# Two ends of an attention and expert kernel: the first projections and the last group rearranged

## The chip, the cores and the metric

The kernel runs on one core of one Trainium2 chip. Its engines are TensorE (PE, with its weight loads as PEld), VectorE (DVE), ScalarE (ACT), GpSimd (POOL) and SyncE (SP), which only issues transfers. ACT and POOL issue transfers too. The metric is the device time of one execution in microseconds; the time before is 2715.6 us, the median of three runs (2714.85 to 2717.81). All times below are microseconds unless marked ns.

## The reference

For 32 sequences of 512 tokens and 256 channels, 16 heads of 16 channels, causal attention runs twice. The values are the input itself. The second attention takes its values from the first one's error.

```python
qk = x @ W_attn + b_attn
q, k = (qk[..., :C], qk[..., C:])          # v = x, by heads
y = _causal_attn(q, k, v)
e = v[:, :, 1:, :] - y[:, :, :-1, :]
k2 = (x[:, :-1] @ W_k2 + b_k2)
y2 = _causal_attn(q[:, :, 1:, :], k2, e)   # a row of zeros ahead
x = layernorm(x + proj(y) + proj(y2))
x = layernorm(x + ffn(x))                  # ffn: top-2 of 8 experts
```

The experts touch only the first 512 tokens, sequence 0. For the other 31 sequences the expert output added is nought, so the second norm follows the first directly.

## The kernel before

**Tiling.** Four heads make a group, four groups a sequence: 128 groups in all. Two neighbouring groups are projected together (`project`, L194 to L213): the products land in a PSUM bank, ACT adds a bias and writes `pk` (L210), POOL rounds it to `lead` (L212) and subtracts (L213), so that `lead` and `pk` hold a high and a low part. `spread` (L215) moves both to the layout of the score products, `q_t` and `kk_t`, by SBUF-to-SBUF transfers of 128 KB or halves of that on SP's queue.

**Steps.** `step(n)` (L631) is a pipeline over groups. It runs five slots. A slot multiplies queries and keys for the maxima of group n (`maxima`, reduced by DVE at L296), and for the exponentials of group n-1 (`scores`, exp by ACT at L353, the causal triangle cut by POOL at L357). After each slot come the functions in `rest[slot]`: `values` (products `av` at L400, drained by ACT at L408), `normalize` (transposes `yt` at L415, the division by DVE, and for the first attention POOL's `e_pad` at L440), projections of a later pair, the output projection (`turn` and `attended`, products `po` at L492), the experts of sequence 0, and loads and stores. `values(n, 0)` and `normalize(n, 0)` are the first attention of a group, `(n, 1)` the second.

**The last block.** For every sequence but 0, `attended(b, i)` adds the residual to block i of 128 rows (DVE, L495) and calls `twice_normed`: statistics by DVE (L507, L508), the factor r by POOL (L510, L511), the norm itself by POOL (L512). `store(b)` (L515) writes all four blocks as one transfer of 512 KB, eight steps after the sequence's end, or for the last sequence in step 131.

**What sets the order.** The instructions of PE and SP stand in the order of the code. Those of DVE, ACT and POOL are ordered by a scheduler when the kernel is built, and each engine then runs strictly in that order. In the start this has a consequence: the small work of `route` for the experts (load of `rws` by POOL at L526, `wt * rws` by DVE at L536) stands ahead of DVE's first maximum. PSUM has four single banks (`bank`) and two double ones; a new tile waits until the one that held its bank has been drained.

**Before the steps.** SP loads `xT` and the weights, ACT issues eight small bias loads (L102), `w_proj` and `b_proj`; DVE packs the weights (L108); POOL builds masks. Then pair 0 is projected and spread, the first x and its shifted copy xs are loaded (L175 to L183), and POOL makes two tiles of ones (L708, L712).

Of the kernel before, what the change touches and what calls it, by code (L numbers as in the profile page):

```python
# [9 lines left out]
F32 = mybir.dt.float32  # L10
# [3 lines left out]
AF = mybir.ActivationFunctionType  # L14
ALU = mybir.AluOpType
AX = mybir.AxisListType

P = 128
# [16 lines left out]
def half(ap):  # L35
    return ap.bitcast(F32R)
# [3 lines left out]
def block_kernel(  # L40
# [16 lines left out]
    nc = tc.nc  # L57
    B, T, C = x.shape
# [9 lines left out]
    const = ctx.enter_context(tc.tile_pool(name="const", bufs=1))  # L68
# [10 lines left out]
    def bank(name):  # L79
        return psum.tile([P, T], F32, tag="one", name=name, bufs=4)  # L80


    seqs = {}

    def load_turned(b):
# [82 lines left out]
    moving = {}  # L168

    def load(b):  # L170
        if b:
            load_turned(b)
        s = seqs[b]
        s["x"] = seq.tile([P, NB, C], F32, tag="x", name=f"x{b}")
        nc.sync.dma_start(s["x"], x[b].rearrange("(n p) c -> p n c", p=P))  # L175
# [18 lines left out]
    def project(two, m, lo=0, hi=T):  # L194
        b, part = divmod(two, NG // 2)
        ps = bank(f"pj{two}_{m}_{lo}")
        for c in range(NC):
            nc.tensor.matmul(  # L198
                ps[:, 0 : hi - lo],
                wq_sb[:, m, c, part * P : (part + 1) * P],  # L200
                seqs[b]["xT"][:, c, lo:hi],
                start=(c == 0),
                stop=(c == NC - 1),
            )
        if lo == 0:
            pk = work.tile([P, T], F32, tag=f"half{m}", name=f"pk{two}_{m}", bufs=1)
            lead = work.tile([P, T], F32, tag=f"lead{m}", name=f"lead{two}_{m}", bufs=1)
            moving[two, m] = lead, pk
        lead, pk = moving[two, m]
        nc.scalar.activation(pk[:, lo:hi], ps[:, 0 : hi - lo], AF.Identity, bias=bp_qk[:, m, part : part + 1])  # L210
        if hi == T:
            nc.gpsimd.tensor_copy(half(lead), pk)  # L212
            nc.gpsimd.tensor_sub(half(pk), pk, lead)  # L213

    def spread(two, m):  # L215

        for k in range(2):
            n = 2 * two + k
            d = groups.setdefault(n, {})
            d["q"] = q_t[n % len(q_t)]  # L220
            d["kk"] = kk_t[n % len(kk_t)]
            rows = slice(k * GH * HD, (k + 1) * GH * HD)
            for i, t in enumerate(moving[two, m]):
                if m == 0:
                    for r in range(2):
                        nc.sync.dma_start(d["q"][r::2, i], t[rows])
                else:
                    nc.sync.dma_start(d["kk"][i::2, m - 1], t[rows])
        del moving[two, m]

# [159 lines left out]
    def values(n, a):  # L392
        b, g = divmod(n, NG)
        d = groups[n]
        vals = (v_pad, e_pad)[a]
        ps = bank(f"av{n}_{a}")
        order = [0, 2, 1, 3] if a == 0 else [0, 1, 3, 2]
        for j in order:
            for h in range(GH):
                nc.tensor.matmul(  # L400
                    ps[HS * h : HS * (h + 1), j * P :],
                    vals[:, j, (g * GH + h) * HV : (g * GH + h) * HV + HS],
                    d["pt", a, j, h // NH2][:, h % NH2],
                    start=(j == order[0]),
                    stop=(j == order[-1]),
                )
        avs = d["avs", a] = work.tile([P, T], F32, tag="avs", name=f"avs{n}_{a}")
        nc.scalar.copy(avs, ps)  # L408
# [75 lines left out]
    def attended(b, i):  # L484

        s = seqs[b]
        if i == 0:
            pool = seq if b else const
            s["h"] = pool.tile([P, NB, C], F32, tag="h" if b else "h0", name=f"h{b}")
        ps = bank(f"po{b}_{i}")  # L490
        for c in range(NC):
            nc.tensor.matmul(  # L492
                ps[:, 0:C], s["ysT"][:, c, i * P : (i + 1) * P], wp_sb[:, c], start=(c == 0), stop=(c == NC - 1)
            )
        nc.vector.tensor_add(s["h"][:, i], ps[:, 0:C], s["xr"][:, i])  # L495
        if b:
            twice_normed(b, i)
        elif i == NB - 1:
            norm(s["h"], f"a{b}")

    def twice_normed(b, i):


        t = seqs[b]["h"]
        mv = small.tile([P, 2], F32, tag="mv2", name=f"mv{b}_{i}")
        stats = small.tile([P, nc.vector.BN_STATS_DIM], F32, tag="stats", name=f"st{b}_{i}")
        nc.vector.bn_stats(stats, t[:, i])  # L507
        nc.vector.bn_aggr(mv, stats)  # L508
        r = small.tile([P, 1], F32, tag="r2", name=f"r{b}_{i}")
        nc.gpsimd.tensor_scalar(r, mv[:, 1:2], 1.0 + EPS, EPS * EPS, ALU.mult, ALU.add)  # L510
        nc.gpsimd.tensor_tensor(r, r, mhalf[:, 0:1], ALU.pow)  # L511
        nc.gpsimd.tensor_scalar(t[:, i], t[:, i], mv[:, 0:1], r, ALU.subtract, ALU.mult)  # L512

    def store(b):
        nc.sync.dma_start(out[b].rearrange("(n p) c -> p n c", p=P), seqs.pop(b)["h"])  # L515
# [112 lines left out]
    n_all = B * NG  # L628
    first_expert = 2 * NG + 4

    def step(n):  # L631
        ready = lambda k: 0 <= k < n_all
        rest = [[] for _ in units]
        b, r = divmod(n, NG)
        if r == 1 and b + 1 < B:
            load(b + 1)
        if r == 3 and b + 1 < B:
            load_next(b + 1)
        if ready(n):
            prepare(n)  # L640
        if ready(n - 3):
            rest[3].append(lambda: normalize(n - 3, 1))
        if ready(n):
            rest[4].append(lambda: halve(n))
        if ready(n - 1):
            rest[0].append(lambda: augment(n - 1))
        if ready(n - 2):
            rest[1].append(lambda: values(n - 2, 0))
            rest[2].append(lambda: normalize(n - 2, 0))
            rest[4].append(lambda: values(n - 2, 1))  # L650
        two = n // 2 + 1
        if ready(2 * two):
            if n % 2 == 0:
                rest[2].append(lambda: project(two, 1))
                rest[4].append(lambda: spread(two, 1))
            else:
                rest[2] += [lambda: project(two, 0), lambda: spread(two, 0)]
                rest[0].append(lambda: project(two, 2, 0, T // 2))
                rest[3] += [lambda: project(two, 2, T // 2), lambda: spread(two, 2)]
        b, r = divmod(n - 3, NG)  # L660
        if r == NG - 1 and 0 <= b < B:
            rest[4].append(lambda b=b: turn(b))

        for b in range(B):
            end = (b + 1) * NG - 1
            last = b == B - 1
            for part in range(2):
                if n == (end + 4 if last else min(end + 5 + 2 * part, n_all)):
                    rest[0].append(lambda b=b, part=part: attended(b, 2 * part))
                    rest[3].append(lambda b=b, part=part: attended(b, 2 * part + 1))  # L670
                if n == (end + 3 if last else end + 4):
                    rest[1 + 2 * part].append(lambda b=b, part=part: biased(b, part))
            if n == (end + 2 if last else end + 3):
                rest[3].append(lambda b=b: load_residual(b))
            if b and n == (end + 4 if last else end + 8):
                rest[4 if last else 1].append(lambda b=b: store(b))


        e = n - first_expert
        if e == -1:  # L680
            rest[4] += [route, turn_tokens, lambda: load_hidden(0), lambda: load_down(0)]
        if e == 0:
            rest[0].insert(0, biases)
        if 0 <= e < E:
            rest[3].insert(0, lambda: hidden(e, 0, 0))
            rest[4].insert(0, lambda: hidden(e, 0, 1))
        if 0 <= e - 1 < E:
            rest[0].insert(0, lambda: hidden(e - 1, 1, 0))
            rest[1].insert(0, lambda: hidden(e - 1, 1, 1))
            rest[2].insert(0, lambda: down(e - 1))  # L690
            if e < E:
                rest[1].append(lambda: load_hidden(e))
                rest[2].append(lambda: load_down(e))
        if e == E:
            rest[4].append(lambda: second_norm(0, moe["acc"]))
        for s in range(len(units)):
            slot(n, s)
            for f in rest[s]:
                f()

    for m in range(3):
        project(0, m)
        spread(0, m)
    load(0)
    load_next(0)
    for a in range(2):
# [85 lines left out]
```

## Time and profile before

| | |
|---|---|
| median of the runs | 2715.6 |
| profiled execution, its own time | 2717.53 |
| its span | 2715.8 |
| PE busy | 2618.0 (96%) |
| DVE busy | 1933.8 (71%) |
| ACT busy | 1754.0 (65%) |
| POOL busy | 1733.0 (64%) |
| chain that ended last | PE 76%, ACT 14%, issue 3%, POOL 3%, DVE 2%, DMA 1% |

The span runs from the first to the last instruction; the profiled execution took 1.7 us longer than its span. The chain follows the work back from the last instruction to what released each step. A timeline line gives start, duration, engine and line, operation, output and input, and in brackets how long the engine had been idle and what ended it. "PEclk" is the clock that PE was granted, 1.00 being full.

### The profile page before, as it was taken

The numbers are of one execution on the slowest core, as the hardware profiler recorded it, in microseconds if no ns is written. First come the engines' busy times: TensorE is split into PE (matmuls) and PEld (weight loads), VectorE is DVE, ScalarE is ACT, GpSimd is POOL, SyncE is SP. The second block draws the span as 40 slices with busy tenths as digits, with TensorE's granted clock in tenths as the row PEclk, the third lists the DMA queues.
The fourth block names the chain that finished last, engine by engine and source line by source line (L and its number), as shares of the span: only waits on it lengthen the run. The fifth ranks groups of instructions, "written<-read, shape, count | busy, mean of one in ns | idle before, by whom it ended". The sixth has DMA issues, their size and how long they took to land.

```text
span 2715.8 us, 98001 instructions
## 1 busy us (share of the span) xinstructions
PE 2618.0 (96%) x41488; PEld 1786.1 (66%) x41488; DVE 1933.8 (71%) x3220; ACT 1754.0 (65%) x3412; POOL 1733.0 (64%) x3312
## 2 busy tenths in 40 slices
PE   6999999999999999999999999999999999999996
PEld 3666666666666666666666666666666666666664
DVE  5767777777777777777777777777777777777772
ACT  2666554566666666666666666666666666666663
POOL 4555555566666666666666666666666666666665
PEclk7999999999999999999999999999999999999998
DMA  5233223233233333333333333333333333333320
GB/s 137 70 74 99 68 86 89 77 80 101 81 85 90 87 96 80 97 85 80 95 85 97 80 100 83 78 97 85 98 80 97 86 78 97 84 99 79 97 55 24
DMA packets 166421, 233.25 MB, mean 86 GB/s; under 512 B 20472, under 2 KB 90112, under 8 KB 165984
## 3 DMA queue, kind: packets, MB, share of 16 engines
q1 hardware_dynamic: 164544, 226.54, 31.8%
q8 instruction: 329, 5.39, 0.8%
q14 instruction: 108, 0.88, 0.1%
q10 hardware_dynamic: 1312, 0.40, 0.1%
q0 software_dynamic: 128, 0.05, 0.0%
HBM read 75.41 MB, written 16.78 MB: 34 GB/s over the span
## 4 chain that ended last, share of the span: by engine, by line
PE 76%; ACT 14%; issue 3%; POOL 3%; DVE 2%; DMA 1%; ACTq 0%; POOLq 0%; SPq 0%; DVEq 0%
PE av L400 22%; PE sc L336 15%; ACT pt L353 12%; PE pj L198 11%; PE sm L272 8%; PE sm L257 5%; PE yt L415 5%; PE po L492 4%; PE mt L309 3%; PE gu L584 2%; POOL lead L212 1%; PE dn L607 1%; DVE top L296 1%; ACT pk L210 1%; PE ys L481 1%
## 5 line engine op out<-in xcount | busy, mean ns | idle before, releaser
L296 DVE TENSOR_REDUCE top<-sm 128x2 f32<-128x768 f32 (+3 forms) x1800 | 1536.3, 907 | 658.7 <-PE sm L272 658.3
L353 ACT ACTIVATE pt<-sc 128x512 f32<-128x512 f32 (+1 forms) x2564 | 1322.5, 603 | 388.7 <-PE sc L336 215.4
L357 POOL TENSOR_SCALAR_AFFINE_SELECT pt<-pt 128x256 f32<-128x256 f32 x2048 | 786.3, 407 | 572.9 <-ACT pt L353 571.9
L272 PE MATMUL sm<-kk_t,q_t 32*128 32x512 f32 (+2 forms) x7168 | 1105.2, 380 | 24.0 <-DVE top L296 15.3
L336 PE MATMUL sc<-q_t,kk_t 32*128 32x256 f32 (+3 forms) x8192 | 1028.3, 337 | 5.2 <-DVE h L495 2.1
L336 PEld LDWEIGHTS sc<-q_t,kk_t 32*128 32x128 f32 x8192 | 668.3, 184 | 276.4 <-issue 160.9
L336 PE MATMUL sc<-m,minus 32*128 32x256 f32 (+3 forms) x4096 | 671.9, 318 | 0.0
L272 PEld LDWEIGHTS sm<-kk_t,q_t 32*128 32x128 f32 x7168 | 567.0, 185 | 30.8 <-DVE top L296 11.6
L257 PE MATMUL sm<-hide,pick 32*128 32x64 bf16 (+5 forms) x10240 | 516.7, 217 | 0.0
L336 PEld LDWEIGHTS sc<-m,minus 32*128 32x128 f32 x4096 | 411.1, 184 | 9.7
L198 PE MATMUL pj<-xT,wq_sb 128*128 128x256 f32 (+1 forms) x1020 | 398.9, 514 | 6.1 <-DVE wq_sb L108 6.1
L408 ACT COPY avs<-av 128x512 f32<-128x512 f32 x256 | 150.2, 587 | 323.0 <-PE av L400 323.0
L400 PE MATMUL av<-pt,e_pad 128*32 128x512 f32 (+3 forms) x4096 | 302.2, 435 | 23.4 <-ACT pt L353 14.3
L400 PE MATMUL av<-pt,v_pad 128*32 128x512 f32 (+3 forms) x4096 | 304.9, 438 | 16.5 <-POOL pt L357 3.4
L210 ACT ACTIVATE pk<-pj,bp_qk 128x256 f32<-128x256 f32 (+1 forms) x255 | 151.2, 593 | 192.8 <-PE pj L198 192.8
L400 PEld LDWEIGHTS av<-pt,v_pad 128*32 128x32 f32 x4096 | 137.5, 110 | 185.3 <-issue 135.3
L213 POOL TENSOR_TENSOR pk<-pk,lead 128x512 fp32r<-128x512 f32 x192 | 244.7, 1275 | 10.6
L257 PEld LDWEIGHTS <-pick 32*128 32x128 bf16 x10240 | 242.9, 93 | 1.2 <-issue 0.7
L400 PEld LDWEIGHTS av<-pt,e_pad 128*32 128x32 f32 x4096 | 130.4, 109 | 165.2 <-issue 158.4
L198 PEld LDWEIGHTS pj<-xT,wq_sb 128*128 128x128 f32 x1020 | 175.9, 192 | 92.6 <-issue 64.9
L415 PE MATMUL yt<-ident,avs 128*128 128x128 f32 x1024 | 167.7, 287 | 7.4 <-ACT pt L353 1.9
L444 POOL TENSOR_TENSOR y<-y,y 128x256 f32<-128x256 f32 x128 | 96.3, 752 | 122.5 <-DVE mv L508 73.3
(88 smaller groups left out, 1958.3 us busy)
## 6 DMA issues: line engine op xcount, KB each, us to landing
q_t<-lead SPq DMA_DIRECT2D x256, 128.0 KB
q_t<-pk SPq DMA_DIRECT2D x256, 128.0 KB
kk_t<-lead SPq DMA_DIRECT2D x256, 128.0 KB
kk_t<-pk SPq DMA_DIRECT2D x256, 128.0 KB
xT<-in_xT SPq DMA_DIRECT2D x32, 512.0 KB
x<-in_x SPq DMA_DIRECT2D x32, 512.0 KB
xr<-in_x SPq DMA_DIRECT2D x32, 512.0 KB
out<-h SPq DMA_DIRECT2D x32, 512.0 KB
```

What stands on the lines that cost most here:

```text
L198: nc.tensor.matmul(ps[:, 0 : hi - lo], wq_sb[:, m, c, part * P : (part + 1) * P], seqs[b]["xT"][:, c, lo:hi], start=(c == 0), stop=(c == N ...
L210: nc.scalar.activation(pk[:, lo:hi], ps[:, 0 : hi - lo], AF.Identity, bias=bp_qk[:, m, part : part + 1])
L213: nc.gpsimd.tensor_sub(half(pk), pk, lead)
L257: nc.tensor.matmul(ps[hh][:, 0 if alone else hh].rearrange("p (k c) -> p k c", c=P)[:, first::step, HS * c :], pick[rows, c], hide[rows, c ...
L272: nc.tensor.matmul(part(ps[hh], i, na, at)[:, 0 if alone else hh], half(d["q"][rows, k, i * P : (i + 1) * P]), half(d["kk"][rows, a : a + ...
L296: nc.vector.tensor_reduce(to, view, AX.X, ALU.max)
L336: nc.tensor.matmul(ps[hh][:, at * P : at * P + T - j * P], half(keys), half(queries[:, j * P :]), start=(k == 0), stop=(k == 2),)
L353: nc.scalar.activation(pt[:, hh, lo:hi], ps[hh][:, lo:hi], AF.Exp, scale=HD**-0.5)
L357: nc.gpsimd.affine_select(diag, diag, pattern=[[0, NH2], [1, P]], compare_op=ALU.is_ge, fill=0.0, base=-a, channel_multiplier=-1,)
L400: nc.tensor.matmul(ps[HS * h : HS * (h + 1), j * P :], vals[:, j, (g * GH + h) * HV : (g * GH + h) * HV + HS], d["pt", a, j, h // NH2][:, ...
L408: nc.scalar.copy(avs, ps)
L415: nc.tensor.transpose(ps[:, i * P : (i + 1) * P], d["avs", a][:, i * P : (i + 1) * P], ident)
```

## The change

A one-element tile `early` is set to nought and run through Exp ahead of everything else, which brings the load of ACT's function table there. For pair 0 the rounding to `lead` moves from POOL to ACT. `spread` can take one of the two groups; for pair 0 all transfers of group 0 are issued ahead of those of group 1. In step 129 `values(127, 0)` comes after slot 0 instead of slot 1, and `normalize(127, 0)` after slot 1 instead of slot 2. In step 131 the four blocks of the last sequence are projected in the order 0, 1, 2, 3 (before 0, 2, 1, 3); their norm runs on DVE, and each block is stored by itself. The stores of the other sequences keep their step; that of sequence 30 falls in step 131 too, where its place on SP's queue is now behind the four single stores.

```diff
+    early = const.tile([P, 1], F32, name="early")
+    nc.vector.memset(early, 0.0)
+    nc.scalar.activation(early, early, AF.Exp)
     seqs = {}
...
         if hi == T:
-            nc.gpsimd.tensor_copy(half(lead), pk)
+            if two:
+                nc.gpsimd.tensor_copy(half(lead), pk)
+            else:
+                nc.scalar.copy(half(lead), pk)
             nc.gpsimd.tensor_sub(half(pk), pk, lead)
 
-    def spread(two, m):
-
-        for k in range(2):
+    def spread(two, m, which=range(2)):
+
+        for k in which:
...
-        del moving[two, m]
+        if 1 in which:
+            del moving[two, m]
...
-        nc.gpsimd.tensor_scalar(t[:, i], t[:, i], mv[:, 0:1], r, ALU.subtract, ALU.mult)
+
+        by = nc.vector if b == B - 1 else nc.gpsimd
+        by.tensor_scalar(t[:, i], t[:, i], mv[:, 0:1], r, ALU.subtract, ALU.mult)
+        if b == B - 1:
+            nc.sync.dma_start(out[b, i * P : (i + 1) * P], t[:, i])
...
-            rest[1].append(lambda: values(n - 2, 0))
-            rest[2].append(lambda: normalize(n - 2, 0))
+            soon = n > n_all
+            rest[0 if soon else 1].append(lambda: values(n - 2, 0))
+            rest[1 if soon else 2].append(lambda: normalize(n - 2, 0))
             rest[4].append(lambda: values(n - 2, 1))
...
-                    rest[0].append(lambda b=b, part=part: attended(b, 2 * part))
-                    rest[3].append(lambda b=b, part=part: attended(b, 2 * part + 1))
+                    for i in range(2 * part, 2 * part + 2):
+                        rest[0 if last or i % 2 == 0 else 3].append(lambda b=b, i=i: attended(b, i))
...
-            if b and n == (end + 4 if last else end + 8):
-                rest[4 if last else 1].append(lambda b=b: store(b))
+            if 0 < b < B - 1 and n == end + 8:
+                rest[1].append(lambda b=b: store(b))
...
     for m in range(3):
         project(0, m)
-        spread(0, m)
+        spread(0, m, [0])
+    for m in range(3):
+        spread(0, m, [1])
     load(0)
     load_next(0)
```

## The prediction

> **What bounds the kernel now.** I read the page's busy shares first: TensorE (PE) has work in 96% of the span, and the slices are level between the first and the last. The change leaves every engine's order between the first projections and step 129 as it was, so what can move lies in the first 30 us and the last 40. I then read the chain of work that ended last in these two stretches, and the engines' timelines beside it. The start, by the chain (start, length in us, what):
>
> ```profile
> 6.14 6.43 PE pj L198 x8
> 12.60 0.69 ACT pk L210
> 13.34 0.61 POOL lead L212
> 13.96 2.66 POOL pk L213 x2
> ...
> 25.23 5.36 DMA rws<-in_rw
> 30.69 0.19 DVE wt L536
> 30.89 2.40 DVE top L296 x4
> ```
>
> The first maxima do not wait for the first group's transfers. They stand on VectorE (DVE) behind `wt * rws`, which waits for the load of `rws`. GpSimd (POOL) issues that load only after its projection work and the two `ones` tiles. PE did the first scores early and then stood still (stretch, PE busy, weight loads, DVE, ACT, POOL, granted clock, DMA share):
>
> ```profile
> 20.00:25.40 5.40, 3.14 (x56) 2.24 (x56) 0.40 (x2) 0.00 (x0) 4.66 (x15) 0.50 0.92 208
> 25.40:32.20 6.80, 0.01 (x2) 0.04 (x2) 3.06 (x15) 0.00 (x0) 3.25 (x8) 0.50 0.46 155
> ```
>
> ScalarE (ACT) in the start, by its timeline:
>
> ```profile
> 10.34 1.28 ACT L210 ACT_TABLE_LOAD   x1 [10.34 <-DMA wide<-in_w_qkk]
> 11.64 0.69 ACT L210 ACTIVATE pk<-pj,bp_qk 128x512 f32<-128x512 f32 x1
> ...
> 14.31 0.69 ACT L210 ACTIVATE pk<-pj,bp_qk 128x512 f32<-128x512 f32 x1 [1.03 <-PE pj L198]
> ```
>
> The third `pk` starts when PE ends pj at 14.27, whatever happens before it. The end, by the chain:
>
> ```profile
> 2684.29 4.06 PE av L400 x32
> ...
> 2691.57 0.73 POOL e_pad L440
> 2692.34 2.40 PE av L400 x32
> ...
> 2701.47 0.44 DVE h L495
> ...
> 2707.71 0.56 POOL r L511
> 2708.37 1.22 POOL h L512
> ```
>
> The last group goes scores, `av`, `e_pad`, `av`, then POOL norms four blocks one after another to 2711.83. The store is issued at 2711.86 and the span ends at 2715.8, 3.94 later.
>
> **The change, part by part.** The sum is made against the profiled span, 2715.8 (that run took 2717.5 in all, 1.7 around it; the runs' median is 2715.6, so I carry the difference over to the median).
>
> *Early table load: 0.* It takes 1.28 off the head of the first `pk`. That load waited for the last of eight bias loads, issued at 6.66 and in by 10.34, 3.7 later. In the changed order the table load and a one-element Exp come after the first bias load, so bias loads 2 to 8 are issued some 1.5 later (1.28 and about 0.2). Four of them also wait for a semaphore that an earlier load must free: the waits of before show 3.8 to 4.5 us from issue to freed. So the last is issued at about 8.0, lands at 11.7, and `pk` starts where it did (11.64); bounds 10.8 and 12.6. [...]
>
> *Rounding by ACT: -1.25 at the start.* Three casts leave POOL (0.61 to 0.67 each) and three copies come to ACT. The nearest row is ACT's own cast `m`, 128x512, 0.617. ACT then runs 11.65 pk, 12.40 lead, 13.05 pk, 13.80 lead, 14.45 pk, lead to 15.80. POOL subtracts (1.26 to 1.43 each) at 13.05, 14.45 and 15.85, ending 17.15 where it ended at 18.60: 1.45 sooner. Then come both memsets (0.20 each; one stood before the last subtraction), 16 selects (two runs of 2.70), the issue of `ids` (1.05), and `rws` at 24.0 in place of 25.23. Its 5.36 I keep: it shares the DMA engines with x and xs, which SP issues a good half microsecond sooner too. One stretch of xs moves at 24 GB/s from 29.5 to 36, and the few packets of `rws` on that engine trickle beside it. First maxima at 29.6 in place of 30.9. Bounds: 0 (`rws` lands no sooner) and 3 (it gets ahead of x).
>
> *First group's transfers ahead: 0.* Of 16 issues of 0.6 before x, group 0's eight now stand first. The first scores waited for the tenth issue (19.79, product at 22.22: 2.43); it is now the sixth. SP's first two q issues wait for slots of `wp` and `bp2`, loads that ACT now issues about 1.4 later, so I put them at 13.6 and 14.5, the sixth at 16.9, and the first scores at 19.3: 3 us sooner. That gain is hidden by the wait for `rws`: PE stands from about 22.5 instead of 25.4. Without that wait it would be worth 3. Group 1's eight end at 23.5, and step 1 needs them only after 44.
>
> *Last values sooner: -1.9.* `values(127, 0)` moves ahead of the scores of slot 1 and `normalize` ahead of those of slot 2. Its bank comes free at 2680.95. Two of its four key blocks need POOL's `pt4` selects, which stand behind 2.50 of bias adds and end at 2682.82, so 32 products (2.40) end at 2683.85. Then `avs` 0.59 to 2684.5; slot 1's scores, whose fourth bank is that of `av`, 1.1 to 2685.6; its exps free a bank for `yt` at 2686.25; `y` at 2687.66; `e_pad`, on POOL behind a pair of selects, 2687.75 to 2688.47; the remaining selects to 2690.1, the last needed only by the last key block; `yt` of group 126 to 2689.45, and there the second `av` starts, instead of at 2692.34: 2.9 sooner, if PE keeps its clock.
>
> Against that speaks the clock, by stretches of 3.4 us (columns as above):
>
> ```profile
> 2680.90:2684.30 3.40, 2.40 (x26) 1.52 (x27) 0.00 (x0) 2.28 (x6) 2.64 (x7) 1.00 0.15 50
> 2684.30:2687.70 3.40, 3.40 (x24) 1.31 (x28) 0.00 (x0) 1.31 (x3) 1.53 (x4) 0.50 0.00 0
> ```
>
> PE's clock fell to half at 2684.3 and came back 3.4 later; the first `av` paid for it, 4.06 instead of 2.40. [...]
>
> *Norms by DVE: -2.3.* From the first `h` add (0) POOL's last norm ended at 10.36: per block r 0.19, pow 0.56, norm 1.22, with gaps 2.23. DVE does the same norm in 0.41 (L458, 128x256). But DVE keeps order, and each norm stands before the next block's statistics: norm 0 waits for POOL's r until 2.4, then come the aggregate of block 1 and add 2; norm 1 at 3.9; add 3 is pushed to 4.7; norm 2 at 6.2, norm 3 at 7.7 to 8.1. That is 2.3 sooner. PE's po products (0.87 a block) are hidden.
>
> *Single stores: +0.4.* The store of sequence 30 (512 KB) used to go out at 2678.95. Now its step comes after the four single stores on SP's queue, so it is issued last, 0.4 after the last single one. Its data still need 1.5 and its landing the rest of 3.94. Had it not been moved, a last store of 128 KB would save 1.1.
>
> Sum: 0 - 1.25 + 0 - 1.9 - 2.3 + 0.4 = -5.05: 2710.5.
>
> **Rivals.** *More of it holds:* `rws` lands ahead of x (-3) and PE stays warm (-2.9), with -1.9 at the stores: -7.8, 2707.8. [...] Against: the same DMA queue is full then. *Less of it holds:* the bias loads come in late (12.6), `rws` is no sooner (0), the second `av` is cold (-0.8) and the tail is -1.6: -2.4, 2713.2. For it: each gain is behind a second wait that the trace shows. *Slower:* the four-byte tile `early` is allocated first and moves every later SBUF tile up by 32 bytes, as the built program has it. If that cost the steady steps anything, it would come 128 times: from 84 ns a step (0.4% of 20.6 us) the whole is slower by 0.2%, 10.8 over 128 steps against a gain of 5.05. I put 2722 there. Against: operands are whole rows of 512 B to 2 KB, and nothing in the trace tells one tile's address from another's. *It does not do what it says:* for the early table load and the transfers this is part of my forecast.
>
> **How the numbers follow.** Forecast 0.45, more 0.24, less 0.26, slower 0.05. A measurement here tells about 0.2%, 5.4 us, so the line is 2710.2, just below the forecast, whose own range is 2708.8 to 2712. A little under half of its chance lies on the fast side; with "more", and nothing of "less", that is near 0.47 faster, 0.48 same, 0.05 slower. Range 2705.5 to 2714.5 takes in "more" and "less" with the 1.5 by which runs differ.
>
> **What would show it.** The chain at the start still goes through the load of `rws`, issued near 24.0, and the first maxima start at 29 to 30; first scores near 19.3; first `pk` near 11.6. At the end: second `av` of group 127 some 8 after POOL's last bias add (11.0 before, 2681.38 to 2692.34), at half or full clock; DVE's last norm ends about 8.1 after the first `h` add (10.36 before), and there are five stores of which the last is 512 KB. It is wrong if the first maxima come before 28, if the `av` starts less than 1 sooner, or if the steps between have another length.

## The result, and the profile after

The changed kernel takes 2709.55 us (median of 11 runs, 2707.0 to 2710.92). The kernel before, on the same chip, takes 2715.94 (11 runs, 2714.39 to 2719.69). The ratio of the runs is 0.9974, with a 95% interval of 0.9965 to 0.9984: faster by 0.26%. The profiled execution has a span of 2708.5, against 2715.8 before. Where these 7.3 lie is read from five points that both traces have:

| stretch | before | after | difference | forecast |
|---|---|---|---|---|
| start of the span to the first maxima | 30.80 | 29.70 | -1.1 | -1.25 |
| first maxima to POOL's last bias add (steps 0 to 129) | 2650.6 | 2648.0 | -2.6 | 0 |
| last bias add to the first `h` add of the last block | 20.09 | 17.54 | -2.55 | -1.9 |
| first `h` add to the last norm | 10.36 | 8.59 | -1.8 | -2.3 |
| last norm to the end of the span | 3.98 | 4.67 | +0.7 | +0.4 |

The chain of waits at the start, of the kernel after (start, length, what):

```profile
6.13 6.55 PE pj L202 x8
12.71 0.69 ACT pk L214
13.43 0.63 ACT lead L219
...
15.84 1.26 POOL pk L220
...
22.87 1.01 POOL ids L534
23.89 5.48 DMA rws<-in_rw
29.41 0.05 issue
29.46 0.32 DVE wt L548
29.78 2.41 DVE top L304 x4
```

It is the chain of before with POOL's casts gone. POOL issues `rws` at 23.89 in place of 25.23, and the load takes 5.48 as it took 5.36. The first score products, before and after:

```profile
22.22 0.80 PE L272 MATMUL sm<-kk_t,q_t 32*128 32x384 f32 x8 [7.95 <-DMA kk_t<-pk]
19.16 0.80 PE L280 MATMUL sm<-kk_t,q_t 32*128 32x384 f32 x8 [4.78 <-DMA kk_t<-pk]
```

They start 3.06 sooner, and then PE stands, as this stretch of the kernel after shows (stretch, its length, then the busy time of PE, weight loads, DVE, ACT and POOL, the granted clock, the DMA share and GB/s):

```profile
24.30:31.10 6.80, 0.02 (x2) 0.05 (x2) 3.16 (x14) 0.00 (x0) 2.99 (x8) 0.50 0.60 162
```

ACT's timeline in the same place, after:

```profile
1.51 1.28 ACT L86 ACT_TABLE_LOAD   x1 [1.51 <-PEq L798]
...
9.95 0.69 ACT L214 ACTIVATE pk<-pj,bp_qk 128x512 f32<-128x512 f32 x1 [6.94 <-PE pj L202]
...
14.42 0.69 ACT L214 ACTIVATE pk<-pj,bp_qk 128x512 f32<-128x512 f32 x1 [0.38 <-PE pj L202]
```

The table load stands at 1.51, under the loads of the weights. The first `pk` comes at 9.95, released by PE's product and not by a bias load; the third `pk` still waits for PE.

The chain at the end, after:

```profile
2677.38 2.53 PE av L408 x32
...
2686.02 3.29 PE av L408 x32
...
2694.32 2.56 PE po L500 x6
2696.91 0.42 DVE h L503
...
2701.93 0.41 DVE h L522
...
2703.38 0.41 DVE h L522
```

POOL's last bias add ends at 2677.66 here, and at 2681.38 before. The second `av` starts 8.29 after it (before 10.96), but takes 3.29 instead of 2.40. The first `av`, which took 4.06 before, takes 2.53. The last norm, now on DVE, ends at 2703.79.

### The profile page after: what moved, and what is told of

It reads as the page before. It is cut to its first block, busy times and chain, and to the rows that moved or that the text cites. A ratio compares the mean times of both kernels' runs of the same rounds, so it can differ in the third digit from the quotient of the medians.

```text
span 2708.5 us, 98012 instructions
## 1 busy us (share of the span) xinstructions
PE 2617.6 (97%) x41488; PEld 1785.1 (66%) x41488; DVE 1933.0 (71%) x3225; ACT 1756.6 (65%) x3416; POOL 1725.9 (64%) x3305
## 4 chain that ended last, share of the span: by engine, by line
PE 77%; ACT 14%; issue 3%; POOL 3%; DVE 2%; DMA 1%; ACTq 0%; POOLq 0%; SPq 0%; DVEq 0%
PE av L408 22%; PE sc L344 15%; ACT pt L361 12%; PE pj L202 11%; PE sm L280 8%; PE sm L265 5%; PE yt L423 5%; PE po L500 4%; PE mt L317 3%; PE gu L596 2%; POOL lead L217 1%; DVE top L304 1%; PE dn L619 1%; PE ys L489 1%; ACT pk L214 1%
## 5 line engine op out<-in xcount | busy, mean ns | idle before, releaser
L280 PE MATMUL sm<-kk_t,q_t 32*128 32x512 f32 (+2 forms) x7168 | 1105.3, 380 | 22.6 <-issue 8.8
```

The lines of the kernel that those rows point to most:

```text
L280: nc.tensor.matmul(part(ps[hh], i, na, at)[:, 0 if alone else hh], half(d["q"][rows, k, i * P : (i + 1) * P]), half(d["kk"][rows, a : a + ...
```

## The experiments

The theory to be tested: at the start the load of `rws` is the bound and hides the transfers ahead and the early table load; at the end each gain has the size of a wait that was shortened, and the clock decides how much of the second `av`'s earlier start is kept. The rivals: one end made the whole gain; the shift of all tiles costs the steps; the table load or the transfers gained something by themselves.

All sizes in one table. "First scores" and "maxima" are starts in the profile. "To `av` 2" and "to `h`" are counted from the end of POOL's last bias add; then come the length of the second `av`, the time from the first `h` add to the end of the last norm, and from there to the end of the span. The ratio is to the kernel before on the same chip.

| kernel | median | ratio, 95% interval | first scores | maxima | to `av` 2, its length | to `h` | norms | tail |
|---|---|---|---|---|---|---|---|---|
| before | 2715.94 | 1 | 22.22 | 30.80 | 10.96, 2.36 | 20.09 | 10.36 | 3.98 |
| after | 2709.55 | 0.9974 (0.9965-0.9984) | 19.16 | 29.70 | 8.29, 3.31 | 17.54 | 8.59 | 4.67 |
| start alone | 2715.08 | 0.9985 (0.9976-0.9993) | 20.03 | 26.93 | 11.23, 3.87 | 20.90 | 10.37 | 3.97 |
| end alone | 2713.93 | 0.9986 (0.9977-0.9995) | 22.34 | 30.46 | 8.44, 3.00 | 17.67 | 8.60 | 4.69 |
| after, `rws` early | 2701.67 | 0.9939 (0.9927-0.9952) | 19.95 | 21.77 | 8.59, 4.45 | 19.82 | 7.77 | 4.68 |
| before, `rws` early | 2710.59 | 0.9967 (0.9955-0.9980) | 24.56 | 26.38 | 10.91, 2.36 | 20.03 | 11.19 | 3.98 |
| after, store of 30 ahead | 2709.18 | 0.9967 (0.9955-0.9980) | 19.40 | 26.33 | 8.49, 4.50 | 19.76 | 7.94 | 3.00 |
| `rws` early, store ahead | 2702.82 | 0.9942 (0.9930-0.9955) | 18.87 | 20.69 | 8.61, 4.47 | 19.85 | 7.80 | 2.99 |
| the same, memsets later | 2702.94 | 0.9941 (0.9927-0.9954) | 19.48 | 21.29 | 8.58, 4.47 | 19.84 | 7.77 | 3.00 |
| before, shift alone | 2718.14 | 0.9999 (0.9990-1.0008) | 22.56 | 31.06 | 10.85, 2.36 | 19.99 | 11.18 | 3.98 |
| products in the gap | 2697.99 | 0.9931 (0.9918-0.9943) | 18.80 | 20.62 | 7.92, 2.36 | 16.07 | 7.76 | 2.99 |
| after, table late | 2713.76 | 0.9986 (0.9977-0.9995) | 19.43 | 30.01 | 8.58, 4.38 | 19.74 | 8.60 | 4.68 |
| `rws` early, transfers in order | 2704.84 | 0.9956 (0.9942-0.9969) | 21.63 | 23.45 | 8.36, 3.10 | 17.61 | 8.62 | 4.68 |
| after, `ids` early | 2706.59 | 0.9964 (0.9951-0.9978) | 19.99 | 25.60 | 8.30, 3.22 | 17.56 | 8.60 | 4.67 |

The kernel before had medians of 2719.18, 2718.01, 2715.57 and 2715.95 on the chips of these runs, so ratios are compared, not medians. Every start and length in the table is of one profiled execution; the medians and ratios are of 5 or 11 executions.

**The two ends apart.** The start alone takes the early `Exp`, the copies on ACT and the new order of transfers, and leaves the end as it was:

```diff
+    nc.scalar.activation(early, early, AF.Exp)
...
+                nc.scalar.copy(half(lead), pk)
...
+        spread(0, m, [0])
+    for m in range(3):
+        spread(0, m, [1])
```

> The three parts at the start alone (early table load, rounding by ACT, first group's transfers ahead), the end as before. [...] Everything after POOL's last bias add as before: 10.96 to the second av, 10.36 from the first h add to the last norm. Rival (the start gave nothing, all of the change's gain is in the end): first maxima near 30.8, 2715.5. Rival (the move of every SBUF tile by 32 bytes costs a steady step something): the halving casts of step 100 later than before in spite of the earlier first maxima.

The end alone takes the rest:

```diff
+            rest[0 if soon else 1].append(lambda: values(n - 2, 0))
+            rest[1 if soon else 2].append(lambda: normalize(n - 2, 0))
...
+        by = nc.vector if b == B - 1 else nc.gpsimd
...
+            nc.sync.dma_start(out[b, i * P : (i + 1) * P], t[:, i])
```

> The parts at the end alone (last values sooner, last norms by VectorE, single stores), the start as before. My theory: first maxima at 30.8 as before; from POOL's last bias add to the second av of group 127 8.4 instead of 10.96; from the first h add to the last norm 8.6 instead of 10.36; tail 4.7 after it: together -3.5 to -4.5, 2711 to 2712.5. Rival (the gain of the whole change came from the start and the steps between): -1 or less, 2714.5 or more. Together with the start alone the two gains should make the -6.4 measured for the whole, within the 1.5 by which runs differ.

Both gain: 0.15% and 0.14%, some 4 us each, which together is near the 0.26% of the whole. That one end made everything falls. (The three edits of the end, and the rounding by ACT, were not run one by one; what each is worth is read from the profiles.) The end alone came out as said (8.44, 8.60, 4.69). The start alone did not repeat the start of the kernel after: its first maxima came at 26.93, not near 29.70. Its chain of waits shows why:

```profile
22.20 0.25 POOL ones L721
22.45 2.93 DMA ids<-in_idx
...
26.82 0.19 DVE wt L543
27.01 2.41 DVE top L303 x4
```

The load of `rws`, issued at 23.5, took 2.7 instead of 5.5. In this execution SP issued the load of `x` at 24.2, behind it; in the profile after, SP had issued `x` at 23.3 and POOL `rws` at 23.9. The code of the two starts is the same. With the short load the chain no longer goes through `rws` but through the load of `ids` and DVE's small work on it (25.41 to 26.82), so not all of the time saved on the load comes through. A new theory follows: the load of `rws` is short when it is issued ahead of `x`, and which comes first is a race between two queues.

**The race, tested by moving one issue.** POOL sends off the 4 KB of `ids` before the projections, so that its issue (1.05) no longer stands ahead of that of `rws`:

```diff
     for t in (v_pad, e_pad):
         nc.gpsimd.memset(t, 1.0)
+    ids = const.tile([P, NB, 2], I32, name="ids")
+    nc.gpsimd.dma_start(ids, idx.rearrange("(n p) k -> p n k", p=P))
...
-        ids = const.tile([P, NB, 2], I32, name="ids")
-        nc.gpsimd.dma_start(ids, idx.rearrange("(n p) k -> p n k", p=P))
```

> The changed kernel with one issue moved: POOL sends off the 4 KB load of ids before the projections instead of just ahead of rws, so that rws is issued 1.05 sooner (22.5 to 23.0), mostly ahead of SP's load of x (23.3 to 24.2 in the profiles so far). My theory (rws takes 2.6 to 2.7 when its issue stands before that of x and 5.2 to 5.6 when behind it): rws in 2.5 to 2.9, first maxima at 25.5 to 26.5, which is 3.2 to 4.2 sooner than in the profile of the changed kernel for an issue that moved by 1.05; 2705 to 2708. Rival (the load's length is chance, or its own queue's): 5.2 or more, first maxima at 28.2 to 28.8, 2708 to 2709.5.

The chain of waits of this kernel:

```profile
22.64 2.75 DMA rws<-in_rw
25.49 0.19 DVE wt L548
25.68 2.41 DVE top L306 x4
```

`rws` is issued at 22.6, `x` at 24.3, and the load takes 2.75: the first maxima start 4.1 sooner than after, for an issue that moved by 1.3. (The ratio, 0.9964 against 0.9974, points the same way, but the intervals overlap.) In all profiles in which `rws` is loaded at its old place, the order and the length go together:

| kernel | `rws` issued | `x` issued | `rws` took |
|---|---|---|---|
| before | 25.2 | 24.2 | 5.4 |
| end alone | 25.1 | 24.4 | 5.2 |
| shift alone | 25.6 | 24.6 | 5.3 |
| table late | 24.2 | 23.7 | 5.6 |
| after | 23.9 | 23.3 | 5.5 |
| start alone | 23.5 | 24.2 | 2.7 |
| store of 30 ahead | 22.8 | 23.6 | 2.6 |
| `ids` early | 22.6 | 24.3 | 2.8 |

The change brings the two issues near enough that executions of one start fall on either side. The profiled execution of the kernel after fell on the slow side. How many of the 11 timed runs did is not known.

**The wait for `rws` taken away.** Both loads go ahead of the projections. The two copies of `minus`, which stand on DVE ahead of the first maxima and need POOL's late tiles of ones, go to ACT. First in the kernel after:

```diff
+    ids = const.tile([P, NB, 2], I32, name="ids")
+    nc.gpsimd.dma_start(ids, idx.rearrange("(n p) k -> p n k", p=P))
+    rws = const.tile([P, NB, E], F32, name="rws")
+    nc.gpsimd.dma_start(rws, rw.rearrange("(n p) e -> p n e", p=P))
...
-        nc.vector.tensor_copy(half(minus[a]), ones[:, 0:P])
+        nc.scalar.copy(half(minus[a]), ones[:, 0:P])
```

> The changed kernel, and in addition the wait that bounded its start is taken away: POOL issues ids and rws ahead of the first projections instead of behind its selects, and ACT instead of DVE copies the two minus tiles, which also stood on DVE behind POOL's late tiles of ones. My theory (the wait for rws is the bound, and the transfers ahead are hidden behind it): first maxima at 20 to 23 right behind the first scores, PE's stand of 8.8 before its next projection goes to 2 or less, and 6 to 9 less in all: 2701 to 2704. Rival (the loads of x and xs, or the maxima's own work on DVE, are late too): first maxima sooner, but the next wait (a load, the tiles of ones for group 0's values) gives it back within steps 1 and 2; 2707 to 2710.

Then the same two edits in the kernel before, whose transfers go by turns and whose table load is late:

> The kernel before with the same two edits as the run beside it (ids and rws issued early, minus by ACT), its transfers in the old order and its table load late. My theory: first scores at 22.2 as before, or some 0.5 sooner, first maxima just behind them at 23 to 24, 2708 to 2711. Against the changed kernel with the same edits, the first maxima stand 3 later: that is what the transfers ahead, nothing behind the wait for rws, are worth when it is gone. Rival (transfers ahead are worth nothing even then): first maxima of the two within 1 of each other.

The chain of waits of the first of the two:

```profile
17.14 2.57 DMA kk_t<-pk
19.70 0.25 issue
19.95 0.80 PE sm L286 x8
...
21.78 2.48 DVE top L310 x4
```

The maxima now start 1.8 after the first scores, and these wait for the transfers of `kk_t`: what was hidden is the bound. The time falls to a ratio of 0.9939, a gain of 0.61% where the change has 0.26%; the two intervals do not overlap. PE's first projection of the next pair starts at 26.10 where it started at 34.03. From the first maxima to the last bias add it takes 2650.6, as the kernel before does, so nothing of it is given back against that one.

In the kernel before the same edits bring the maxima to 26.38, but its first scores came at 24.56, two later than expected. In both of these profiles DVE's first copy of a weight was slow, which the last section takes up; PE's first product starts 2.6 late in both. Between the two, scores and maxima differ by 4.6, of which the rounding on ACT is a part.

**The transfers by themselves.** The kernel with `rws` early, with the order of transfers of before:

```diff
-        spread(0, m, [0])
-    for m in range(3):
-        spread(0, m, [1])
+        spread(0, m)
```

> The kernel with rws early and minus by ACT (2701.7 when it ran), with the transfers of the first pair back in the order of before: group 0 and 1 by turns. My theory (with the wait for rws gone the transfers ahead are worth what they were said to hide): first scores and first maxima 2.5 to 3.5 later, measured from the third pk, 2703.5 to 2706 in all. Rival (they are worth nothing: something else holds the first scores): within 1 of it.

First scores at 21.63 and maxima at 23.45. The two profiles with the transfers ahead whose projection also began at 6.1 and that share the place of the memsets had scores at 18.87 and 18.80, maxima at 20.69 and 20.62, so the order is worth 2.8 where the wait is gone. The ratio is 0.9956 against 0.9939, with intervals that overlap, so the size rests on the profiles.

**The table load by itself.** The kernel after, without the `Exp` on `early`:

```diff
-    nc.scalar.activation(early, early, AF.Exp)
```

> The changed kernel without the Exp on early, so that the load of ACT's table stands again in front of the first pk; the tile itself stays. My theory (the early table load is worth nothing): first pk at 11.3 to 11.7 instead of 9.95, the third pk tied to PE's product as before (14.3 to 14.5), first maxima in one of the two places that its start has had (26.3 to 27, or 29.3 to 30.2, by whether the load of rws or that of x is issued first), same time as the changed kernel within 1.5. Rival (the table load is a part of the gain): third pk and POOL's last subtraction 1 or more later, 1.3 to 2.5 slower than the changed kernel.

ACT's timeline:

```profile
10.26 1.28 ACT L213 ACT_TABLE_LOAD   x1 [10.26 <-DMA wide<-in_w_qkk]
11.55 1.26 ACT L213 ACTIVATE pk<-pj,bp_qk 128x512 f32<-128x512 f32 x2
12.71 1.14 ACT L218 CAST lead<-pk 128x512 fp32r<-128x512 f32 x2
13.73 0.70 ACT L213 ACTIVATE pk<-pj,bp_qk 128x512 f32<-128x512 f32 x1
```

and POOL's subtractions behind it:

```profile
13.40 3.96 POOL L219 TENSOR_TENSOR pk<-pk,lead 128x512 fp32r<-128x512 f32 x3 [4.80 <-ACT lead L218]
```

The load is back ahead of the first `pk`, and the third `pk` here has no wait in brackets: it stands behind ACT's own two `pk` and two casts. PE's last product of the three had been done at 12.97, 0.76 earlier. So the load is not always hidden: with the rounding on ACT, ACT is the later one when PE is quick. The late load also holds back the first `lead`, and the three subtractions then run back to back to 17.36, where they end at 17.10 after, although PE's products were done 1.4 sooner here. The first maxima come 0.3 later than after (30.01 against 29.70). The ratio, 0.9986 against 0.9974, would make the load worth 3 us, more than the rival's 1.3 to 2.5, but the intervals overlap: by the timed runs anything from nothing to a few microseconds is left open. This execution also had the slow kind of second `av` (below) and lost the race at 24.2 to 23.7. Whether the late table makes the race be lost more often is open.

**The shift.** The kernel before with only the tile `early`:

```diff
+    early = const.tile([P, 1], F32, name="early")
+    nc.vector.memset(early, 0.0)
```

> The kernel before with only the four-byte tile early allocated first and set to nought by DVE, without its Exp: all later SBUF tiles move up by 32 bytes, nothing else changes. My theory: same time within 0.2%, steps of the same length. Rival (the shift costs the steady steps from 84 ns each): 5.4 or more slower.

The ratio is 0.9999 (0.9990 to 1.0008). From the first maxima to the last bias add it took 2651.3 against 2650.6. That is the longest of the 14 profiles, but only 5 ns a step, where the rival needs 84. The rival falls.

**The last store.**

```diff
-            if 0 < b < B - 1 and n == end + 8:
+            if 0 < b < B - 1 and n == min(end + 8, n_all + 2):
```

> The changed kernel with the store of sequence 30 one step sooner (step 130 instead of 131), so that it is no longer behind the four single stores on SP's queue. My theory (the 0.4 lost at the tail is that store's place): the last store is one of 128 KB, last norm to the end of the span 3.1 to 3.6 instead of 4.71, 1.1 to 1.5 less in all. Rival (the tail is the latency of any store): 4.3 or more, no gain that can be measured.

SP's timeline at the end of the kernel after:

```profile
2698.81 5.34 SPq L524 DMA_DIRECT2D out<-h  x4
2704.24 0.39 SPq L527 DMA_DIRECT2D out<-h  x1
```

and of this kernel:

```profile
2673.46 0.38 SPq L527 DMA_DIRECT2D out<-h  x1
2698.61 5.35 SPq L524 DMA_DIRECT2D out<-h  x4
```

The 512 KB go out at 2673.46, under other work, and the tail is 3.00 instead of 4.67: 1.7 less, a little more than expected. The median shows little of it (2709.18), and its ratio of 0.9967 has an interval that holds 0.9974.

**Both of these together, and the memsets.** `rws` early and the store ahead:

> The changed kernel with rws issued early and minus copied by ACT (as in the run above with 2701.7), and the store of sequence 30 one step sooner. Expected if the two gains add up: first maxima at 20 to 23, tail 3.1 to 3.6, 2699.5 to 2701.5. Rival (the end hides one in the other): 2702 or more.

In a further kernel the memsets of `v_pad` and `e_pad` come behind the two loads on POOL:

```diff
-    for t in (v_pad, e_pad):
-        nc.gpsimd.memset(t, 1.0)
     ids = const.tile([P, NB, 2], I32, name="ids")
...
+    for t in (v_pad, e_pad):
+        nc.gpsimd.memset(t, 1.0)
```

> As the run beside it, and POOL's memsets of v_pad and e_pad come behind the issue of ids and rws instead of ahead of it. In the two runs with rws early, DVE's first copy of a weight ran from 6.01 to 8.70, across those memsets of POOL (6.48 to 8.54), and PE's first product started at 8.75 instead of 6.14. Theory (DVE's copy is held up while POOL writes these tiles): first product at 6.1 to 6.5, third pk and first scores 1 to 2.5 sooner, 1 to 2 less in all than the run beside it. Rival (the weights landed late by chance and POOL has no part in it): first product near 8.7 as before, or 6.1 in both runs, no difference between the two.

The two are alike: 0.9942 and 0.9941, tails of 2.99 and 3.00. Together with the store ahead, `rws` early was no faster than without it (0.9939), and its median of 2702.82 lies where the rival had it (2702 or more). Yet the tail is 1.7 shorter in the profiles; such a difference is inside the intervals, so the times do not show that the two gains add up. For PE's start the pair says nothing about the memsets: the weights landed by 5.7 in both, and PE started at 6.14 in both. What it does show of them stands in the last section.

**The clock at the end.** The nine profiles above with the last values sooner fall into two kinds. In four the second `av` took 3.0 to 3.3 and the first `h` add came 17.5 to 17.7 after the last bias add. In five it took 4.4 to 4.5, and the `h` add came at 19.7 to 19.9, where the kernel before has 20.1. To see whether the clock does this, 15 products that nobody reads were put between the two `av`, and ahead of `ys`, in the kernel with `rws` early and the store ahead:

```diff
+    def keep_warm(count):
+        ps = pair_of_banks("warm")
+        for k in range(count):
+            nc.tensor.matmul(ps[:, k % NH2], pick[:, 0], hide[:, :, k % 4, :], start=True, stop=True)
...
+        if n == n_all + 1:
+            rest[0].append(lambda: keep_warm(2))
+            rest[1].insert(0, lambda: keep_warm(3))
+            rest[1].append(lambda: keep_warm(3))
+            rest[2].append(lambda: keep_warm(3))
+        if n == n_all + 2:
+            rest[4].insert(0, lambda: keep_warm(4))
```

> The kernel with rws early, minus by ACT and the store of sequence 30 ahead, and in addition 15 bf16 products of 128x128 by 128x512 whose result nobody reads, in the gaps of PE between the two av of group 127 (11) and between yt and ys (4). In the four profiles of kernels with the last values sooner where the second av was at half clock throughout it took 4.45 to 4.50 and POOL's last bias add stood 19.8 before the first h add; in the two where it took 3.0 and 3.3, 17.6. [...]

Stretches at the end without the products (PE busy, weight loads, DVE, ACT, POOL, granted clock, DMA share, GB/s):

```profile
2673.10:2676.50 3.40, 2.43 (x33) 1.70 (x29) 0.23 (x1) 2.16 (x5) 0.42 (x2) 1.00 0.00 0
2676.50:2679.50 3.00, 2.44 (x16) 1.64 (x15) 0.45 (x2) 1.70 (x5) 2.37 (x6) 0.59 0.01 3
2679.50:2684.00 4.50, 4.50 (x33) 1.39 (x32) 0.85 (x3) 0.39 (x1) 0.98 (x2) 0.52 0.00 0
```

and with them:

```profile
2668.90:2672.30 3.40, 2.79 (x46) 1.64 (x42) 0.00 (x0) 0.58 (x1) 1.73 (x5) 1.00 0.00 0
2672.30:2675.70 3.40, 3.40 (x27) 1.78 (x26) 0.68 (x2) 2.48 (x6) 1.89 (x5) 1.00 0.00 0
2675.70:2679.10 3.40, 3.04 (x38) 1.39 (x36) 0.85 (x3) 1.41 (x5) 1.86 (x4) 1.00 0.03 7
```

Without them the clock is at 0.59 ahead of the second `av` and at 0.52 in it, although PE had been busy for 2.43 of the 3.40 before that. With them it stays at 1.00, the second `av` takes 2.36, and the first `h` add comes 16.07 after the last bias add, 3.8 sooner than in the kernel beside it: the clock stays at 1.00 behind the second `av` too, to 2682.50, and the second `ys` takes 0.66 instead of 1.12. The products themselves delay nothing that can be seen. This is the fastest kernel of the study: 2697.99 us, ratio 0.9931 (0.9918 to 0.9943), 17.6 below the kernel before beside it. It beats both kernels. Against the one without the products, 0.9942, the intervals overlap, and only one profile of each tells what the products are worth: from the last bias add to the end of the span 26.8 instead of 30.7.

## Why the prediction was right, point by point

The total was forecast at 2710.5 and came out at 2709.55, but the sum of the profile is -7.3 where -5.05 was forecast. The terms stand in the first table.

*Early table load: 0.* The step's reason was wrong. The bias loads were not issued 1.5 later: the last one went out at 7.03, where it went out at 6.66 before. The first `pk` came at 9.95, ahead of the bound of 10.8, and PE's product was what it waited for. (With the early load it came at 10.28 with the products in the gap, at 10.49 with the transfers in order, at 10.65 with the store of 30 ahead, and, with late weights, at 12.56 in the kernel after with `rws` early.) The early load gave nothing at the third `pk`, which waited for PE, as the prediction says of the kernel before. But this tie holds only when PE is the later one; with the table late ACT was later by 0.76, so nought is right for this execution and not for all. The one table load that the kernel has costs its own 1.28 and no more: with the table late the load ends at 11.54 and `pk` starts at 11.55.

*Rounding by ACT: -1.25.* Right in the profiled execution: `rws` at 23.89 (24.0 said), first maxima at 29.70 (29.6 said), by the steps given. "Its 5.36 I keep" was a choice between two outcomes and not a value with a margin: the upper bound, "it gets ahead of x", comes about with 2.6 to 2.8 for the load and maxima at 25.6 to 26.9, in three of the five profiles with this rounding and `rws` loaded behind the projections. The reason given for keeping it, that SP issues `x` sooner too, held in the profile after (`x` at 23.3, before 24.2); in those three `x` was issued at 23.6 to 24.3, behind `rws`.

*First group's transfers ahead: 0.* Right: first scores at 19.16 (19.3 said), hidden by the wait for `rws`. "Without that wait it would be worth 3": measured 2.8. Even a short load of `rws` still hides it, for the maxima then start at 25.6 or later.

*Last values sooner: -1.9.* The mechanism is right, the second `av` 2.7 sooner (2.9 said). No run shows the 1.9, which was the author's estimate between an `av` that keeps its clock and one that does not. The runs show two cases in its place: to the first `h` add the gain is 2.3 to 2.6 with an `av` of 3.0 to 3.3, and only 0.1 to 0.4 with one of 4.4 to 4.5 (against the 20.0 to 20.1 that three of the four with the old order show; the fourth, the start alone, had 20.9 and no `av` at full clock). The nine together average about -1.2: the forecast of -1.9 was too large, and the profiled execution had the better kind. Nor does a run show the -0.8 of the rival with a cold `av`: such an `av` left 0.1 to 0.4. Five of nine profiles had the slow kind. In the rows above, half clock followed a stretch in which PE was busy for 2.43 of 3.40. That the clock is the cause is shown by the products in the gap (clock 1.00 and an `av` of 2.36, against 0.52 and 4.47 without them); what chooses the kind is not shown, for the code of these profiles does not differ there.

*Norms by DVE: -2.3.* 8.59 where 8.1 was said. "PE's po products are hidden" is the step that was off: after, the second `h` add waited 0.82 for `po`, and from 2695.2 to 2696.9 the clock was at 0.50. The profiles have two lengths on each side: 7.8 to 7.9 or 8.6 with DVE's norms, 10.4 or 11.2 with POOL's. Like with like the move is worth 2.6, but before had the short kind and after the long one, so 1.8 remained. The two places are tied: of the nine profiles, all four with the quicker second `av` have norms of 8.6, and four of the five with the slower one 7.8 to 7.9, so some 0.8 of what a quick `av` gains is given back there.

*Single stores: +0.4.* +0.7, by the cause named: with the store of sequence 30 out of the way the tail falls by 1.7, where the prediction's 1.1 and 0.4 make 1.5.

*The steps between: 0.* The prediction said that it would be wrong if these had another length, and in the profiled execution they had one: 2.6 shorter. No work of the change stands there: DVE, ACT and POOL run the same instructions in the same order through these steps in both traces. Over the 14 profiles the same stretch took 2647.3 to 2651.3, in kernels of both kinds: 2647.3 in the kernel before with `rws` early, 2651.3 with the shift alone, 2650.3 with the end alone. One place accounts for much of it in this pair: between two casts of DVE that each end a step's maxima (`mx`; before at 138.39 and 163.47, after at 137.64 and 160.77) the step is 1.95 shorter. There PE waits for POOL's cut, 3.43 before and 2.79 after, and its clock falls. The stretch before:

```profile
144.80:148.20 3.40, 0.54 (x12) 0.06 (x4) 0.22 (x1) 0.37 (x1) 2.33 (x2) 1.00 0.17 55
148.20:151.60 3.40, 2.83 (x34) 1.57 (x38) 0.00 (x0) 0.58 (x1) 3.37 (x10) 0.50 0.00 0
151.60:155.00 3.40, 3.40 (x45) 3.02 (x36) 2.49 (x3) 2.06 (x4) 0.78 (x3) 0.50 0.01 2
```

and after:

```profile
148.20:151.60 3.40, 3.40 (x61) 2.98 (x50) 1.34 (x2) 1.76 (x4) 2.10 (x7) 0.53 0.00 0
151.60:155.00 3.40, 3.40 (x40) 2.13 (x43) 1.70 (x3) 1.76 (x4) 2.37 (x6) 0.97 0.00 0
```

Half clock for 6.8 before, for about 3.5 after. So of the -7.3 of one pair of profiles some -4.7 belongs to the change, and the timed runs, with an interval of -4.3 to -9.5 (the ratio's, times 2716), cannot tell the two apart. That the forecast of the total came so near is in part luck.

## What to carry to other kernels

When a stall is covered by another wait, take the covering wait away in an experiment: here one small load and two copies, not part of the change, were worth 0.35% on top of the change's 0.26% by the ratios, and made a hidden edit worth 2.8. When two queues issue loads at nearly the same time, do not keep the old duration of the later one: look at the issue times of both, for the order may decide it (2.6 to 2.8 or 5.2 to 5.6 here), and write both outcomes into the range. Where PE waits in a tail, look at its clock too: two profiles here, with and without 15 products that nobody reads in the gaps, differ by 3.8 up to the first `h` add, with the clock at 1.00 and at 0.52 in the second `av`.

## What was not expected of the hardware

A load of 16 KB took twice as long behind a load of 512 KB, which others follow, as ahead of it: 5.2 to 5.6 against 2.6 to 2.8, in eight profiles without exception, though the two are issued on different queues and less than 2 us apart. The traces' DMA records show where the time goes: in the long loads of before and after the first 1 KB packet of `rws` starts 3.26 and 4.09 after the issue, when a short load has landed. The 512 KB load is not the only thing that can do this. In the six profiles with `rws` early it was issued at 7.6 to 9.9, more than 13 ahead of `x` and among the transfers of weights and masks, and took 4.3 to 5.6. Why the packets start late is not shown.

DVE's copy of a weight tile (128x256) takes about 0.3 alone (0.29 at 10.59 in the kernel before, with POOL idle). In the two profiles in which the weights landed at 6.0 instead of 5.5 to 5.8, the first copy took 2.65 and more, as in the chain of waits of the kernel after with `rws` early:

```profile
6.04 2.66 DVE wq_sb L112
8.75 7.34 PE pj L208 x12
```

POOL's two memsets of 128x1148 ran from 6.47 to 8.54 beside it, and the copy ended just behind them. PE's first product slipped from 6.14 to 8.75 by weights that came 0.2 to 0.5 later.

That the memsets hold the copy up is shown by the kernel in which they stand behind the two loads. There they ran from 8.48 to 10.54, and it is the copies of that time that are slow (two here, the second of 0.27):

```profile
7.97 2.92 DVE L112 COPY wq_sb<-wide 128x256 f32<-128x256 f32 x2
```

The first of these ends at 10.70. In the profiles of before, after, the start alone, both kernels with `rws` early and the memsets later, a weight copy was still running when the second memset ended, and it ended 0.15 behind it. It delayed PE's first product only where it was the copy which that product needs.
